# A decoder layer on one core: turning the normalized tokens of self attention through memory and VectorE blocks instead of TensorE turns

## The chip, the cores and the metric

The kernel runs on one core of a Trainium2 chip. The metric is the device time of one execution in microseconds (us). Three runs of the kernel before gave 3795.77, 3797.29 and 3797.58 us, so the median is 3797.29 us. The core's engines are named as in the profile: PE is TensorE (matmuls; PEld are its weight loads), DVE is VectorE, ACT is ScalarE, POOL is GpSimd and SP is SyncE, which issues most DMAs. A name with a q behind it (SPq) is the engine's instruction queue.

## What is computed

One decoder layer on 32 batches of 128 tokens with 512 columns, all in float32: self attention, cross attention and a mixture of experts, each on a layer-normalized input and each added to its input. The change touches the input of self attention alone:

```python
def _layernorm(x, axis=-1, eps=1e-05):
    m = jnp.mean(x, axis=axis, keepdims=True)
    v = jnp.var(x, axis=axis, keepdims=True)
    return (x - m) / jnp.sqrt(v + eps)
...
q = (x @ Wq).reshape(b, t, 2 * H, HD).transpose(0, 2, 1, 3) * scaling
k = (x @ Wk).reshape(b, t, 2 * H, HD).transpose(0, 2, 1, 3)
v = (x @ Wv).reshape(b, t, H, 2 * HD).transpose(0, 2, 1, 3)
scores = jnp.einsum('bhqd,bhkd->bhqk', q, k)
...
x = x + _L0_attn_ref(_layernorm(x, axis=-1), ...)
```

The three products with Wq, Wk and Wv sum over the 512 columns of x. TensorE sums over partitions, so the normalized tokens, which are made with a token on each partition, must be turned until the columns lie on the partitions.

## The kernel before

Self attention is the first of the kernel's stages. It goes over the 32 batches in 64 steps, two for each batch. A step n belongs to the batch and head half steps[n] (at most n // 2 and n % 2) and does, in the order of the program text: the turned maxima and half of the sums of the step before (`turn_maxima`, `sums`), the scores of this step and their row maxima (`maxima`), one quarter of the query and key projections of the next pair of batches (`queries_and_keys(g + 1, k)`, with g, k = divmod(n, 4)), the exponentials of the step before, the weighted values of two steps before, and then in odd steps the value projection of one later batch (`values`) and in even steps the output projection of an earlier one (`leave`).

The input is prepared further ahead. For batch b = 2(g + 2) + k // 2, an even step measures mean and variance (`measure`, L56 to L60 on DVE, L62 and L66 on POOL). The following odd step normalizes it (`normalize`, one ACT instruction, L87), turns it (`turn_in`) and loads the x of batch b + 2 (`load`, L151). So the batches 4 to 31 are turned in the 28 odd steps 1, 3, up to 55. Batches 0 to 3 are turned before the steps begin, in a section whose order is written out by hand. `turn_in` makes four TensorE transposes of 128x128 into a PSUM tile (`turn4`, L95) and copies the result to `hT` on ACT (L207). The tiles `xin`, `h` and `hT` have two buffers each.

PSUM is handed out by `banks`, four tiles in rotation (`psum`, bufs=4). Each request takes the tile that was requested four before, and so waits until that one has been read. An odd step requests, in this order: the turned maxima (L291), two for the scores (L251), one for the projections (L220), two for the exponentials (L308), one for the weighted values (L333), one for the value projection (L238) and one for the turn (L95). An even step has the output projection (L405) in place of the last two.

Behind the hand-written section the order on each engine is made by the tile framework's scheduler from its own estimates, not by the program text alone. The changed program is built by the same scheduler. An engine takes its instructions strictly in that order, and so does the queue of SP, on which an issue that waits holds back all the issues behind it.

The changed parts and their lines are: `turn4` (L89 to L96, shared with cross attention), the weight loads (L168 to L180), `normalize` and `turn_in` (L193 to L207), and the calls of `measure`, `normalize`, `turn_in` and `load` in the hand-written section (L471 to L476) and in the loop over the steps (L507 to L518).

Of the kernel before, what the change touches and what calls it, by code (L numbers as in the profile page):

```python
# [10 lines left out]
F32 = mybir.dt.float32  # L11
# [7 lines left out]
P = 128  # L19
E = 512  # L20
EC = E // P
# [14 lines left out]
class Common:  # L36
# [49 lines left out]

        self.nc.scalar.activation(out, src, AF.Identity, bias=down, scale=rstd)  # L87

    def turn4(self, src, order=range(EC)):  # L89


        tr = self.banks()[:, 0, :].rearrange("p (c x) -> p c x", c=EC)
        cols = src.rearrange("p (c x) -> p c x", c=EC)
        for c, n in enumerate(order):
            self.nc.tensor.transpose(tr[:, c, :], cols[:, n, :], self.ident)  # L95
        return tr  # L96
# [15 lines left out]
            call(*args)  # L112


def self_attention(cm, x, x1_d, Wq, Wk, Wv, Wo, lq1, lk1, lq2, lk2, heads, heads_in, beside):

# [11 lines left out]
    nc, tc, bank = cm.nc, cm.tc, cm.banks  # L130
    B = x.shape[0]
    H, D, G = 16, 32, 2
    CP = 2
    ROW = (16, 0)
    with ExitStack() as ctx:
# [7 lines left out]
        pj2 = early.enter_context(tc.tile_pool(name="a_pj2", bufs=2))  # L143

        xin, xres = {}, {}

        def load(b, queue=nc.sync):

            if b < B:
                xin[b] = pj2.tile([P, E], F32, name="xin")  # L150
                queue.dma_start(out=xin[b], in_=x[b])  # L151
# [10 lines left out]
        for b in range(G):  # L162
            load(b, both[b % 2])
        w = {
            name: (wp if name == "wo" else pj).tile([P, EC, E], F32, name=name)
            for name in ("wk", "wq", "wv", "wo")
        }
        for oc in range(EC):  # L168
            for name, src, queue in (("wk", Wk, nc.sync), ("wq", Wq, both[oc < 2])):
                queue.dma_start(  # L170
                    out=w[name][:, :, ts(oc, P)],
                    in_=src[:, ts(oc, P)].rearrange("(c p) m -> p c m", p=P),
                )
            if oc == 0:
                nc.sync.dma_start(out=heads, in_=heads_in)
        vecs = wp.tile([P, 4, 16], F32, name="lam_vecs")
        for i, src in enumerate((lq1, lq2, lk1, lk2)):
            nc.sync.dma_start(out=vecs[:, i, :], in_=src.partition_broadcast(P))
        for name, src in (("wv", Wv), ("wo", Wo)):
            nc.sync.dma_start(out=w[name], in_=src.rearrange("(c p) m -> p c m", p=P))  # L180

        begun = wp.tile([P, 1], F32, name="a_begun")
        nc.scalar.activation(begun, cm.mhalf[:, 0:1], AF.Exp)
# [1 line left out]
        hT, qT, kz, k1, vs = {}, {}, {}, {}, {}  # L185
        last, last_v = {}, [None]
        h, sc_of, qm, expd, u, o, an = {}, {}, {}, {}, {}, {}, {}

        def measure(b):
            if b < B:  # L190
                h[b] = cm.moments(pj2, xin[b], "a_")

        def normalize(b):  # L193
            if b < B:
                rstd, down = h[b]
                h[b] = pj2.tile([P, E], F32, name="h")
                cm.shifted(h[b], xin.pop(b), rstd, down)

        def turn_in(b):

            if b >= B:
                return
            g, i = divmod(b, G)
            if i == 0:
                hT[g] = pj2.tile([P, EC, G * P], F32, name="hT")
            tr = cm.turn4(h.pop(b))
            nc.scalar.copy(hT[g][:, :, ts(i, P)], tr)  # L207

        def queries_and_keys(g, oc):

# [220 lines left out]
        for b in range(G):  # L431
# [8 lines left out]
            out=causal, in_=causal, compare_op=ALU.is_ge, fill=NEG, base=0,  # L440
# [32 lines left out]
        for b in range(G):  # L473
            turn_in(G + b)
            load(2 * G + b)
        first.close()  # L476
        steps = [(b, cp) for b in range(B) for cp in range(EC // CP)]
        for n in range(len(steps) + 5):
            g, k = divmod(n, 2 * G)
            if n == len(steps) - 2 * G:  # L480
                early.close()
            at = {ago: steps[n - ago] for ago in range(6) if 0 <= n - ago < len(steps)}
            if 1 in at:
                turn_maxima(*at[1])
                sums(*at[1], 0)
            if 0 in at:
                maxima(*at[0])
            queries_and_keys(g + 1, k)
            if 1 in at:
                exponentials(*at[1])  # L490
                sums(*at[1], 1)
            if 2 in at:
                weigh(*at[2])
            if k % 2:
                values(g + 1, k // 2)
            elif 5 in at:
                leave(at[5][0])
            if 2 in at:
                divide(*at[2])
                if at[2][1]:  # L500
                    finish(at[2][0])

            def behind():

                return tc.issue_after(last[at[0]].ins) if 0 in at else nullcontext()

            b = (g + 2) * G + k // 2  # L507
            if k % 2 == 0:
                if 3 in at:
                    with behind():  # L510
                        norms(at[3][0])
                measure(b)
                if 4 in at:
                    load_again(at[4][0])
            else:
                normalize(b)
                turn_in(b)
                load(b + G)  # L518
                if 4 in at:
                    with behind():  # L520
                        scale_out(at[4][0])
                    turn_out(at[4][0])
            if n in beside:
                beside[n]()


class CrossAttention:
# [108 lines left out]
    def measure(self, b):  # L636
        q = self.sided[b, "q", 0] = self.pi.tile([P, E], F32, name="xq0", bufs=2)
        self.scale[b] = self.cm.moments_by_sums(self.pi, self.src[b, "q"], q, "x_")
# [575 lines left out]
class Shared:  # L1214
# [4 lines left out]
    G = 4  # L1219
# [482 lines left out]
def decoder_kernel(  # L1702
# [5 lines left out]
    nc = tc.nc  # L1708
    B = x.shape[0]
# [5 lines left out]
    dram = ctx.enter_context(tc.tile_pool(name="dram", bufs=1, space=DRAM))  # L1715
    psum = ctx.enter_context(tc.tile_pool(name="psum", bufs=4, space=PSUM))
    cm = Common(tc, const, psum)
    heads = const.tile([P, 8], F32, name="heads")
# [5 lines left out]
    half_eid = const.tile([P, 2], I32, name="half_eid")  # L1724

    x1_d = dram.tile([B, P, E], F32, name="x1_d")
    h3_d = dram.tile([T, E], F32, name="h3_d")
    h3T_d = dram.tile([B, P, EC, P], F32, name="h3T_d")
    table_ds = [dram.tile([(NX * B + 2) * P, 2], F32, name=f"table_d{i}") for i in range(2)]
# [6 lines left out]
    with tc.tile_pool(name="x_w", bufs=1, side="right") as x_w:  # L1736
        rest = x_w.tile([P, E], F32, name="rest")
        nc.gpsimd.memset(rest, 0.0)
        routing = Routing(cm, x_w, table_ds, B)
        cross = CrossAttention(cm, x_w, x1_d, x2_d, h3_d, h3T_d, ctx_in, routing)  # L1740
        cross.plan(lambda: s_w.load(), lambda: shared.load(0))
        x_ctx = ExitStack()

        def begin():
            cross.begin(
                x_ctx.enter_context(
                    tc.tile_pool(name="x_in", bufs=2, side="right", reuse_waits="tile")
                )
            )
            cross.advance(7)  # L1750

        n = 2 * B
        beside = {
            12: lambda: cross.load_weights(
                xWq, xbq, xWk, xbk, xWv, xbv, xWo, xbo, cos, sin, rotT, gate_w
            ),
            20: lambda: cross.prepare(heads),
            28: routing.prepare,
            n - 4: begin,
        }  # L1760

        for i, count in enumerate((4, 4, 5, 2, 2, 2, 2)):
            beside[n - 3 + i] = lambda count=count: cross.advance(count)
        self_attention(cm, x, x1_d, aWq, aWk, aWv, aWo, lq1, lk1, lq2, lk2, heads, heads_in, beside)
        s_w_pool = ctx.enter_context(tc.tile_pool(name="s_w", bufs=1, reuse_waits="tile"))
        s_w = SharedWeights(cm, s_w_pool, sw_gate, sw_up, sw_down)
        s_h_pool = ctx.enter_context(tc.tile_pool(name="s_h", bufs=2, reuse_waits="tile"))
        shared = Shared(cm, s_h_pool, h3T_d, sum_d, out)
        x_out = ExitStack()
        p2 = x_out.enter_context(tc.tile_pool(name="x_p2", bufs=2, reuse_waits="tile"))  # L1770
        cross.run(p2)
        x_ctx.close()
        s_pool = x_out.enter_context(tc.tile_pool(name="s_p", bufs=1, reuse_waits="tile"))
        shared.use(s_pool, s_w)
        en = mybir.EngineType
        in_order = {en.PE, en.DVE, en.Activation, en.Pool}
        todo = [lambda: cross.rest(2)] * 34 + [
            lambda: routing.tiles(eid, fresh, rows, used, usual, mixed),
            lambda: routing.halves(half, half_eid),
            lambda: nc.sync.dma_start(out=sum_d[T : T + P, :], in_=rest),  # L1780
        ]

        def between():
            if todo:
                todo.pop(0)()

        EARLY = 3  # L1790
        with tc.manual_schedule(engines=in_order):
            for g in range(EARLY - 1):
                shared.group(g, False, between)
            while todo:
                between()
# [42 lines left out]
    for i in range(2):  # L1838
        b = done // 2
        nc.sync.dma_start(  # L1840
            out=out[ts(i, b)].rearrange("b (p r) e -> (b p) (r e)", r=4),
# [57 lines left out]
```

## Time and profile before

| what | value |
|---|---|
| median of three runs | 3797.29 us |
| the profiled execution | 3800.08 us |
| its span, first to last instruction | 3798.3 us |
| mean granted TensorE clock in it | 0.992 |
| first L257 of step 0 / of step 11 | 40.8 us / 163.3 us |
| last turn (L95) of self attention | about 672 us |
| L95 MATMUL on h in self attention, 128 of them | 273 ns each (median) |
| L207 ACT copy to hT, 32 of them | 574 ns each |
| L87 ACT normalization of xin, 32 of them | 816 ns each |
| L56, L58, L60 DVE moments | 694, 181 and 153 ns each |

The span is the time between the first and the last instruction of one execution; the profiled execution took 1.8 us more than its span and 2.8 us more than the median. Self attention takes about the first 720 us of it. In the views below, a time is the start in us from the beginning of the span, followed by the duration in us; merged rows stand for several instructions (x8), and the bracket at the end gives the idle time before the row on its engine and the instruction that ended it. A float32 matmul of the program appears as two MATMUL rows.

### The profile page before, as it was taken

The numbers are of one execution on the slowest core, as the hardware profiler recorded it, in microseconds if no ns is written. First come the engines' busy times: TensorE is split into PE (matmuls) and PEld (weight loads), VectorE is DVE, ScalarE is ACT, GpSimd is POOL, SyncE is SP. The second block draws the span as 40 slices with busy tenths as digits, with TensorE's granted clock in tenths as the row PEclk, the third lists the DMA queues.
The fourth block names the chain that finished last, engine by engine and source line by source line (L and its number), as shares of the span: only waits on it lengthen the run. The fifth ranks groups of instructions, "written<-read, shape, count | busy, mean of one in ns | idle before, by whom it ended". The sixth has DMA issues, their size and how long they took to land. (4 is left out here: it accounts for less than half of the span.)

```text
span 3798.3 us, 59896 instructions
## 1 busy us (share of the span) xinstructions
PE 3717.0 (98%) x19060; PEld 1967.8 (52%) x19060; DVE 2677.8 (70%) x5402; ACT 2076.4 (55%) x5616; POOL 1917.2 (50%) x2154
## 2 busy tenths in 40 slices
PE   8999999899999999999999999999999999999999
PEld 5666666534444444444445555555555555555444
DVE  4888888877777778787326777777777777776111
ACT  6989998847677676776402444444444444443000
POOL 3555455545777777777424554555555555553000
PEclk9999999999999999999999999999999999999999
DMA  3111110121221111111135565656566665564210
GB/s 113 34 35 35 35 37 30 39 83 49 62 60 42 51 51 51 48 49 40 56 110 169 128 164 134 166 121 164 122 156 142 150 150 141 135 172 81 89 56 33
DMA packets 146548, 340.25 MB, mean 90 GB/s; under 512 B 28976, under 2 KB 33776, under 8 KB 146160
## 3 DMA queue, kind: packets, MB, share of 16 engines
q1 hardware_dynamic: 89408, 227.75, 18.8%
q0 software_dynamic: 55616, 107.79, 15.4%
q8 instruction: 154, 2.52, 0.3%
q14 instruction: 170, 1.39, 0.1%
q10 hardware_dynamic: 1200, 0.79, 0.1%
HBM read 574.59 MB, written 102.17 MB: 178 GB/s over the span
## 5 line engine op out<-in xcount | busy, mean ns | idle before, releaser
L694 DVE TENSOR_REDUCE nm<-ps 128x2 f32<-128x1024 f32 x512 | 610.6, 1214 | 113.2 <-PE ps L690 106.8
L717 ACT ACTIVATE xp<-ps 128x1024 f32<-128x1024 f32 x512 | 505.8, 1021 | 264.5 <-PE ps L690 202.7
L1644 POOL DMA_INDIRECT sum_d<-e_out,e_into x192 | 309.9, 1614 | 562.6 <-ACT e_out L1641 438.4
L713 PE MATMUL ps<-xqn,xk 32*128 32x512 f32 x2048 | 528.9, 621 | 20.7 <-ACT xp L717 19.1
L1637 PE MATMUL ps<-wd,e_guT 128*128 128x512 f32 (+1 forms) x1152 | 526.9, 593 | 0.3 <-ACT e_guT L1627 0.3
L690 PE MATMUL ps<-xk,xq 32*128 32x512 f32 x2048 | 526.9, 631 | 0.1
L1584 DVE STREAM_TRANSPOSE e_xT<-e_xr 64x256 f32<-64x256 f32 x800 | 499.5, 624 | 18.9 <-DMA e_xr<-h_d,e_run_of 10.7
L1609 DVE STREAM_TRANSPOSE e_guT<-e_gu 32x96 f32<-32x96 f32 x1600 | 477.7, 299 | 25.2
L1569 POOL DMA_INDIRECT e_xr<-h_d,e_run_of x400 | 413.8, 1035 | 159.7 <-issue 150.0
L1598 PE MATMUL ps<-wg,e_xT 128*128 128x352 f32 x1536 | 486.7, 459 | 0.0
L1598 PE MATMUL ps<-wu,e_xT 128*128 128x352 f32 x1536 | 485.7, 459 | 0.0
L1627 ACT COPY e_guT<-e_turned 32x96 f32<-32x96 f32 (+1 forms) x1600 | 407.1, 254 | 25.1 <-DVE e_turned L1620 3.9
L1598 PEld LDWEIGHTS ps<-wg,e_xT 128*128 128x128 f32 x1536 | 289.7, 189 | 217.8 <-issue 94.5
L278 ACT ACTIVATE s<-s,a_nm 128x128 f32<-128x128 f32 x1024 | 395.7, 396 | 5.2 <-DVE a_nm L264 5.2
L1598 PEld LDWEIGHTS ps<-wu,e_xT 128*128 128x128 f32 x1536 | 291.8, 190 | 162.6
L1641 ACT ACTIVATE e_out<-ps,e_weight 128x512 f32<-128x512 f32 x200 | 137.4, 687 | 411.8 <-PE ps L1637 409.5
L1637 PEld LDWEIGHTS ps<-wd,e_guT 128*128 128x128 f32 (+1 forms) x1152 | 218.5, 190 | 228.2 <-issue 188.5
L1602 ACT ACTIVATE e_act<-ps 128x352 f32<-128x352 f32 x200 | 92.6, 463 | 412.7 <-PE ps L1598 412.7
L713 PEld LDWEIGHTS ps<-xqn,xk 32*128 32x128 f32 x2048 | 169.0, 184 | 285.5 <-ACT xp L717 124.5
L1603 DVE TENSOR_TENSOR e_gu<-e_act,ps 128x352 f32<-128x352 f32 x200 | 104.1, 521 | 274.6 <-ACT e_act L1602 274.1
L728 PE MATMUL ps<-xp,v 128*32 128x512 f32 x2048 | 233.0, 595 | 7.9 <-ACT xp L717 7.9
L1031 POOL DMA_INDIRECT table_d<-entry,at x192 | 202.4, 1054 | 64.0 <-issue 52.9
(310 smaller groups left out, 5575.4 us busy)
## 6 DMA issues: line engine op xcount, KB each, us to landing
wg<-in_L_ffn_w_gate_dram SPq DMA_DIRECT2D x192, 704.0 KB
wu<-in_L_ffn_w_up_dram SPq DMA_DIRECT2D x192, 704.0 KB
wd<-in_L_ffn_w_down_dram SPq DMA_DIRECT2D x192, 576.0 KB
wd<-in_L_ffn_w_down_dram SPq DMA_DIRECT2D x192, 128.0 KB
xg<-in_L_ffn_w_gate_dram SPq DMA_DIRECT2D x16, 704.0 KB
xu<-in_L_ffn_w_up_dram SPq DMA_DIRECT2D x16, 704.0 KB
xd<-in_L_ffn_w_down_dram SPq DMA_DIRECT2D x16, 576.0 KB
xres<-in_x_dram SPq DMA_DIRECT2D x32, 256.0 KB
```

What stands on the lines that cost most here:

```text
L278: nc.scalar.activation(s[:, j, c, side, :], s[:, j, c, side, :], AF.Exp, bias=nm[n][:, side, at : at + 1], accum_out=sm[n][:, to : to + 1],)
L690: self.nc.tensor.matmul(sc[:, i, :], q[rows, ts(c, P)], k[rows, :], start=True, stop=True)
L694: self.nc.vector.tensor_reduce(at[:, self.ROW[side], 2 * pair : 2 * pair + 2], sc, AX.X, ALU.max, negate=True)
L713: self.nc.tensor.matmul(sc[:, i, :], k[rows, ts(c, P)], q[rows, :], start=True, stop=True)
L717: self.nc.scalar.activation(e, sc, AF.Exp)
L1569: self.cm.nc.gpsimd.indirect_dma_start(out=xr[:, t, :], out_offset=None, in_=self.h3_d.rearrange("t (h f) -> (t h) f", h=self.R), in_offse ...
L1584: self.cm.nc.vector.transpose(to[ts(w, half), :, v], xr[ts(v, half), w])
L1598: nc.tensor.matmul(pgu[lanes, half, 0:M], t[:, c, lanes], w[:, c, :], start=c == 0, stop=c == EC - 1,)
L1609: self.cm.nc.vector.transpose(t[ts(q, 32), :, ts(s, 32)], self.part(q, 3)[ts(s, 32)])
L1627: self.cm.nc.scalar.copy(t[ts(q, 32), 0:n, ts(s, 32)], z[ts(s, 32), q - half, 0:n])
L1637: nc.tensor.matmul(py[lanes], t[:n, c, lanes], wd[:n, c, :], start=c == 0, stop=c == last)
L1644: nc.gpsimd.indirect_dma_start(out=self.sum_d[:, :], out_offset=bass.IndirectOffsetOnAxis(ap=into, axis=0), in_=y[:, :], in_offset=None, b ...
```

## The change

The normalized tokens of batches 4 to 31 no longer go to TensorE to be turned. ACT writes them with the columns in another order: column q*128 + 4f + c goes to place q*128 + 32c + f. That row is stored in a new array in memory, `h_d` (one DMA for each batch, 256 KB), and read back with four DMAs of 64 KB, one for each q, in runs of 128 elements (512 bytes): partition 32q + i of the tile `h_runs` receives the runs of the tokens i, 32 + i, 64 + i and 96 + i. One DVE transpose of 32x32 blocks then gives `hT`, in which partition p holds the columns 4p to 4p + 3 instead of p, 128 + p, 256 + p and 384 + p. The rows of Wk, Wq and Wv are loaded in the same order, and batches 0 to 3, which are still turned on TensorE, read every fourth column. In the loop, the even step now normalizes and sends, and the odd step receives and measures the next batch.

```diff
-    def turn4(self, src, order=range(EC)):
+    def turn4(self, src, order=range(EC), strided=False):
         tr = self.banks()[:, 0, :].rearrange("p (c x) -> p c x", c=EC)
-        cols = src.rearrange("p (c x) -> p c x", c=EC)
+        cols = src.rearrange("p (x c) -> p c x" if strided else "p (c x) -> p c x", c=EC)
...
-                    in_=src[:, ts(oc, P)].rearrange("(c p) m -> p c m", p=P),
+                    in_=src[:, ts(oc, P)].rearrange("(p c) m -> p c m", p=P),
...
-        for name, src in (("wv", Wv), ("wo", Wo)):
-            nc.sync.dma_start(out=w[name], in_=src.rearrange("(c p) m -> p c m", p=P))
+        nc.sync.dma_start(out=w["wv"], in_=Wv.rearrange("(p c) m -> p c m", p=P))
+        nc.sync.dma_start(out=w["wo"], in_=Wo.rearrange("(c p) m -> p c m", p=P))
...
-        def turn_in(b):
-            if b >= B:
-                return
+        def turned(b):
             g, i = divmod(b, G)
             if i == 0:
                 hT[g] = pj2.tile([P, EC, G * P], F32, name="hT")
-            tr = cm.turn4(h.pop(b))
-            nc.scalar.copy(hT[g][:, :, ts(i, P)], tr)
+            return hT[g][:, :, ts(i, P)]
+
+        def turn_in(b):
+            nc.scalar.copy(turned(b), cm.turn4(h.pop(b), strided=True))
+
+        def send(b):
+            if b >= B:
+                return
+            rstd, down = h[b]
+            t = pj2.tile([P, E], F32, name="h")
+            cm.shifted(
+                t.rearrange("p (q c f) -> p q f c", q=4, c=EC),
+                xin.pop(b).rearrange("p (q f c) -> p q f c", q=4, c=EC), rstd, down,
+            )
+            nc.sync.dma_start(out=h_d[b], in_=t)
+            h[b] = pj2.tile([P, 4, P], F32, name="h_runs")
+            for q in range(4):
+                nc.sync.dma_start(
+                    out=h[b][ts(q, 32)],
+                    in_=h_d[b][:, ts(q, P)].rearrange("(t i) r -> i t r", i=32),
+                )
+
+        def receive(b):
+            if b < B:
+                nc.vector.transpose(
+                    turned(b).rearrange("p c (t i) -> p c t i", i=32),
+                    h.pop(b).rearrange("p t (c f) -> p c t f", c=EC),
+                )
...
         for b in range(G):
             turn_in(G + b)
             load(2 * G + b)
+        measure(2 * G)
         first.close()
...
-                measure(b)
+                send(b)
                 if 4 in at:
                     load_again(at[4][0])
             else:
-                normalize(b)
-                turn_in(b)
+                receive(b)
+                measure(b + 1)
                 load(b + G)
...
+    h_d = dram.tile([B, P, E], F32, name="h_d")
```

More of the change, by code (lines that the diff above doesn't have):

```diff
@@ L112, in run, with self_attention @@
             call(*args)
-def self_attention(cm, x, x1_d, Wq, Wk, Wv, Wo, lq1, lk1, lq2, lk2, heads, heads_in, beside):
+def self_attention(cm, x, x1_d, h_d, Wq, Wk, Wv, Wo, lq1, lk1, lq2, lk2, heads, heads_in, beside):
     nc, tc, bank = cm.nc, cm.tc, cm.banks
@@ L1763, in decoder_kernel @@
             beside[n - 3 + i] = lambda count=count: cross.advance(count)
-        self_attention(cm, x, x1_d, aWq, aWk, aWv, aWo, lq1, lk1, lq2, lk2, heads, heads_in, beside)
+        self_attention(cm, x, x1_d, h_d, aWq, aWk, aWv, aWo, lq1, lk1, lq2, lk2, heads, heads_in, beside)
         s_w_pool = ctx.enter_context(tc.tile_pool(name="s_w", bufs=1, reuse_waits="tile"))
```

## The prediction

> **What bounds the kernel now.** I read the page first, for the busiest engine:
>
> ```profile
> PE 3717.0 (98%) x19060; PEld 1967.8 (52%) x19060; DVE 2677.8 (70%) x5402; ACT 2076.4 (55%) x5616; POOL 1917.2 (50%) x2154
> ```
>
> PE is busy 98% of the span, and the chain of waits that ended last is PE work too, but a modelled busy time doesn't say what a step costs. So I read the busy time by stretches of self attention next (start and end, length, then busy us and instructions of PE, PEld, DVE, ACT, POOL, then granted clock, DMA share, GB/s). The first stretch holds steps 0 to 10, the second steps 11 to 54.
>
> ```profile
> 40.00:163.00 123.00, 118.38 (x947) 77.52 (x939) 94.90 (x140) 108.50 (x416) 54.85 (x63) 0.96 0.08 25
> 163.00:661.00 498.00, 497.34 (x4092) 318.15 (x4092) 415.71 (x614) 450.73 (x1712) 258.79 (x260) 1.00 0.11 35
> ```
>
> In the second, PE never pauses, ACT is busy 91% and DVE 83%. The timeline of PE over two steps shows where the time goes, even step first, odd step second:
>
> ```profile
> 406.37 1.17 PE L308 MATMUL ps<-qm,k 32*128 32x128 f32 x32
> ...
> 412.08 0.38 PE L291 MATMUL ps<-ident,a_nm 128*128 128x128 f32 x2
> 412.39 1.15 PE L251 MATMUL ps<-kz,qT 32*128 32x256 f32 x16
> 413.46 1.99 PE L220 MATMUL ps<-hT,wk 128*128 128x256 f32 x8
> ...
> 417.11 1.17 PE L308 MATMUL ps<-qm,k 32*128 32x128 f32 x32
> ...
> 422.82 0.60 PE L95 MATMUL ps<-ident,h 128*128 128x128 f32 x4
> 423.26 0.38 PE L291 MATMUL ps<-ident,a_nm 128*128 128x128 f32 x2
> 423.57 1.79 PE L251 MATMUL ps<-kz,qT 32*128 32x256 f32 x16
> 425.30 1.99 PE L220 MATMUL ps<-hT,wk 128*128 128x256 f32 x8
> ...
> 428.95 1.17 PE L308 MATMUL ps<-qm,k 32*128 32x128 f32 x32
> ```
>
> From L308 to L308 the even step takes 10.74 us and the odd one 11.84. The difference of 1.10 has two parts: the turns move L291 back by 423.26 - 422.82 = 0.44, and from L251 to L220 the odd step takes 1.73 where the even one takes 1.07, so 0.66 of waiting inside work that counts as busy. The ACT timeline says for what:
>
> ```profile
> 423.61 0.57 ACT L242 COPY v<-ps 128x512 f32<-128x512 f32 x1
> 424.07 0.64 ACT L368 ACTIVATE sq<-at 128x512 f32<-128x512 f32 x1
> 424.61 0.57 ACT L207 COPY hT<-ps 128x512 f32<-128x512 f32 x1
> ```
>
> With the turn among the PSUM requests, the second score tile of L251 is the one that the value copy (L242) empties at 424.18, and the tile of L220 is the one that the hT copy (L207) empties at 425.18; L220 starts 0.12 later.
>
> **What a step without the turn costs is in the trace.** The last turn is in step 55. Row maxima (L264) of steps 55 to 59:
>
> ```profile
> 664.38 2.35 DVE L264 TENSOR_REDUCE a_nm<-s 128x8 f32<-128x1024 f32 x2
> 675.81 2.35 DVE L264 TENSOR_REDUCE a_nm<-s 128x8 f32<-128x1024 f32 x2
> 686.96 2.35 DVE L264 TENSOR_REDUCE a_nm<-s 128x8 f32<-128x1024 f32 x2
> 697.68 2.35 DVE L264 TENSOR_REDUCE a_nm<-s 128x8 f32<-128x1024 f32 x2
> 708.47 2.34 DVE L264 TENSOR_REDUCE a_nm<-s 128x8 f32<-128x1024 f32 x2
> ```
>
> Steps 55 and 56 together take 22.58 us, steps 57 and 58, with the same projections but no turn, 21.51. So a turn costs **1.07 us** with its waits, which agrees with the 1.10 above.
>
> **The change part by part.**
>
> *Removed turns, steps 11 to 55.* 23 odd steps at 1.07 are **-24.6 us**. The next tile in line is then that of L220 behind the value copy. Without 0.44 and 0.66, L220 would start at 424.20, and the copy ends at 424.18, driven by the exponentials of the same step: a tie, so the wait is gone to within 0.1. Bounds: 0.44 a step (-10.1) if the bank wait stays, 1.10 (-25.3).
>
> *Steps 0 to 10.* Here the built order of the changed program matters, and the diff alone doesn't show it. Nothing holds the front end back any more except `xin`, since `h` leaves for memory. The scheduler places all moments up to batch 31 ahead of the scores of step 11: 26 instead of the 7 that the trace counts in this stretch. It places 28 normalizations there instead of 7, and the first six receives. DVE gains 19 x (0.694 + 0.181 + 0.153) = 19.5 and 6 transposes of 0.711 (the row L392, same shape, same block transpose) = 4.3, so 94.9 + 23.8 = 118.7 of 123. ACT gains 21 x 0.816 = 17.1 less 6 hT copies of 0.574 = 3.4, so 108.5 + 13.7 = 122.2 of 123. PE, which would save 5 x 1.07 = 5.4 here, isn't the bound of this stretch any more; ACT is. At full ACT use it takes 122.2 (-0.8), at the 90.5% of the second stretch 135.0 (+12). I take the middle, **+6**. Bounds: -5.4 if both engines' work hides, and the slow rival below.
>
> *The normalization itself* keeps 512 elements, but writes neighbours 128 bytes apart. No ACT row does that. Nearest: DVE's reciprocal at L745 reads 128x32 at such a step in 343 ns, and L955 the same count side by side in 353. So I take 0.816, with 1.63 (double) as the upper bound: 28 x 0.816 = +22.8, all inside the full ACT stretch. On this the Trainium skill speaks against the change: "SBUF — State Buffer", section "Door 1: The DMA port swizzle", says that each access crossing to a new 16-byte line pays a penalty, and every write here does. It gives ScalarE no figure; no ACT row here shows it. By the rule the sum would lie toward the upper bound, by the reciprocal rows at zero.
>
> *The DMAs.* Each batch adds a store and four reads to SP's queue, all at 0.33 us an issue (the row of xin): 1.65 a batch against 22.58 in which SP now issues three. A load is read 2.57 us after its issue (406.04 issue of xin, 408.61 its L56), so a batch is back about 2.57 + 4 x 0.33 + 2.57 = 6.5 us after ACT, ahead of its receive in the built order. In the later steps the reads are issued one pair of batches early, some 45 us ahead, so a DVE wait on them costs nothing. Behind a waiting read on SP stand the store of x1 and loads of xin and xres; xres is needed about four steps later, xin is the slow rival's subject. Traffic: 28 x 0.5 MB over some 680 us is 21 GB/s more in a stage that moves 35. Cost 0; if the cover goes, the slow rival.
>
> *The receives in the later steps* (22 x 0.711 = 15.6) replace 19 moments (19.5) on DVE, which was idle 17% anyway. They come in twos right before L293, whose result PE needs 3.6 us after L291; two transposes take 1.4. Cost 0, at worst 11 x 1.4 = +15.6.
>
> *Start.* 16 weight loads on PE now read every fourth column: 141 ns each before, at most doubled +2.3, at least 0; I take **+1**. The value weights come in longer rows: 0.
>
> Sum: -24.6 + 6 + 1 = -17.6, so the profiled 3800.1 would become 3782.5; the median of the runs lies 2.8 below the profiled execution, which gives **3780**.
>
> **Rivals.**
> *The bank wait stays.* If ACT reaches the value copy later than PE reaches L220, only 0.44 a step is saved: -10.1 + 6 + 1 = -3, 3794. For: the tie of 0.02 us. Against: steps 57 and 58. A doubled normalization ends in the same place: 122.2 + 22.8 = 145 against 123 is +22, less 24.6, about 3796. Together 0.20.
> *The run ahead is free.* 28 x 1.07 = -30 from all steps: 3767. For: DVE waits 7.4 us on L291 in step 1. Against: ACT's sum. 0.08.
> *Slower: DVE stands before x that hasn't come.* 26 moments now go through a two-buffer loop of load, moments, POOL, ACT and load, and their loads stand on SP behind stores that wait for ACT.
>
> ```profile
> DVE a_ln_stats L56 <- DMA xin<-in_x_dram: 16.4, 19, 1.1
> ```
>
> In the second stretch each moment already waits 0.86 us (16.4 / 19), harmless at 83% DVE. In the first stretch DVE would have 4.3 to spare. The whole becomes a loss when a moment waits more than (24.6 - 1 + 4.3) / 26 = 1.07 us. At a full load time of 2.57 it is 118.7 + 66.8 - 123 - 23.6 = +39; halfway, 1.8 us each, +19: **3816**. For: the load time is 2.5 times the break-even. Against: with DVE late, loads have landed. 0.15.
> *That it doesn't do what it says:* the built PE order is the old one less 28 groups of four turns, so this is out.
>
> **How the numbers follow.** Forecast 0.57, with its own range 3768 to 3791; rivals 0.20, 0.08 and 0.15 as above. A difference of 0.2% is 7.6 us, which is what I take as the limit of telling: faster means below 3789.7, slower above 3804.9. Faster: 0.55 + 0.08 + 0.02 = 0.65; same 0.20; slower 0.15. For 8 in 10 the range goes from 3767 to 3806: it takes in the free run-ahead and the unchanged cases and leaves out most of the slow one.
>
> **What would show it.** L264 to L264 over two steps at 21.5 us in steps 12 to 54; L251 to L220 at 1.07 in both; no L95 between 60 and 672 us; step 11's scores at 163 + 6 us; the new L87 form at 0.82 us; L56 waits on xin under 1 us each in the first stretch. A row of L87 above 1.2 us, a first stretch over 145 us or any L220 waiting for v would prove me wrong.

## The result, and the profile after

Six runs of the changed kernel gave 3819.77 to 3825.24 us, median 3821.89; six runs of the kernel before beside them gave 3795.77 to 3797.58, median 3796.75. The ratio is 1.0068, with a 95% interval of 1.0055 to 1.0081. So the change made the kernel slower by 0.7%, where the forecast was 3780 and a gain. The profiled execution of after has a span of 3819.8 us, 21.5 more than before. (The medians are 25.1 apart; the profiled execution of before was itself 3.3 us above its median.)

Lines 208 and later of the program have moved. The scores on DVE are now L283 (before L257), the row maxima L290 (L264), the projections L246 (L220), the score matmuls L277 (L251), the exponentials L341 (L315), the value copy L268 (L242). New are the store L219, the reads L222 and the block transpose L230.

From the page of after, its busy times, and from its 40 slices the granted clock:

```profile
PE 3708.7 (97%) x18948; PEld 1960.0 (51%) x18948; DVE 2688.4 (70%) x5430; ACT 2074.8 (54%) x5588; POOL 1918.2 (50%) x2154
PEclk8899999989999999999999999999999999999999
```

PE has 112 matmuls fewer, as the change says (28 batches, four turns each), and is busy 8 us less, yet the span is longer. The sum of the busy times doesn't hold the answer. The busy times by stretches of after do (columns as in the prediction: start and end, length, busy us and instructions of PE, PEld, DVE, ACT and POOL, granted clock, DMA share, GB/s):

```profile
40.00:163.00 123.00, 97.10 (x720) 64.03 (x719) 84.02 (x147) 98.24 (x326) 48.35 (x72) 0.83 0.32 101
222.00:661.00 439.00, 438.33 (x3710) 280.38 (x3708) 376.70 (x530) 391.47 (x1536) 222.36 (x202) 1.00 0.12 36
```

In the first stretch every engine did less than before: PE 97.1 us against 118.4, DVE 84.0 against 94.9, ACT 98.2 against 108.5, and the clock fell from 0.96 to 0.83. Nobody was full; all waited for each other. From 222 us on PE has no pause and the clock is 1.00. The DVE timeline of after dates the steps: L283 marks the scores of steps 0, 3, 6, 7, 10 and 11 here, L290 the row maxima of steps 15 and 54 to 57.

```profile
41.22 2.36 DVE L283 TENSOR_TENSOR s<-ps,causal 128x1024 f32<-128x1024 f32 x2 [5.36 <-PE ps L277]
...
80.28 2.36 DVE L283 TENSOR_TENSOR s<-ps,causal 128x1024 f32<-128x1024 f32 x2 [2.06 <-PE ps L277]
...
121.69 2.35 DVE L283 TENSOR_TENSOR s<-ps,causal 128x1024 f32<-128x1024 f32 x2
142.21 2.35 DVE L283 TENSOR_TENSOR s<-ps,causal 128x1024 f32<-128x1024 f32 x2
...
182.08 2.35 DVE L283 TENSOR_TENSOR s<-ps,causal 128x1024 f32<-128x1024 f32 x2
204.32 2.35 DVE L283 TENSOR_TENSOR s<-ps,causal 128x1024 f32<-128x1024 f32 x2
...
257.87 2.35 DVE L290 TENSOR_REDUCE a_nm<-s 128x8 f32<-128x1024 f32 x2
...
679.37 2.34 DVE L290 TENSOR_REDUCE a_nm<-s 128x8 f32<-128x1024 f32 x2
690.16 2.35 DVE L290 TENSOR_REDUCE a_nm<-s 128x8 f32<-128x1024 f32 x2
700.88 2.35 DVE L290 TENSOR_REDUCE a_nm<-s 128x8 f32<-128x1024 f32 x2
711.67 2.35 DVE L290 TENSOR_REDUCE a_nm<-s 128x8 f32<-128x1024 f32 x2
```

Against the same instructions of before, whose times stand in brackets:

- Step 0 starts 0.4 us later (41.22; 40.83).
- Step 11 starts 41.0 later (204.32; 163.31). So steps 0 to 10 cost 40.6 us more.
- Step 15 has its row maxima 47.0 later (257.87; 210.84): 6.0 more.
- Step 55 has them 25.8 later (690.16; 664.38): steps 15 to 54 gained 21.2, which is **1.06 us for each of the 20 turns** that are gone there.

So the late steps do what was predicted, and steps 0 to 14 lose more than twice as much (46.6). In the late steps the PE timeline of after now shows both kinds of step alike, even step first, odd step second:

```profile
406.82 1.15 PE L277 MATMUL ps<-kz,qT 32*128 32x256 f32 x16
407.90 1.99 PE L246 MATMUL ps<-hT,wk 128*128 128x256 f32 x8
...
411.55 1.17 PE L334 MATMUL ps<-qm,k 32*128 32x128 f32 x32
...
417.57 1.15 PE L277 MATMUL ps<-kz,qT 32*128 32x256 f32 x16
418.67 1.99 PE L246 MATMUL ps<-hT,wk 128*128 128x256 f32 x8
...
422.32 1.17 PE L334 MATMUL ps<-qm,k 32*128 32x128 f32 x32
```

From L277 to L246 it is 1.08 and 1.10 us, and L334 to L334 takes 10.77: the wait for the value copy is gone with the turn.

What the first steps wait for stands in the waits of after from 40 to 222 us (us in total, times, longest):

```profile
DVE a_ln_stats L56 <- DMA xin<-in_x_dram: 43.4, 21, 5.2
...
ACT h L87 <- POOL a_ln_down L66: 23.1, 6, 6.5
```

And one turn of the loop behind these waits, in the timeline of step 2 of after, the engines together:

```profile
65.96 2.35 ACT L87 ACTIVATE h<-xin,a_ln_down,a_ln_rstd 128x512 f32<-128x512 f32 x2
...
67.69 0.42 SPq L151 DMA_DIRECT2D xin<-in_x_dram  x1
...
70.68 0.69 DVE L56 BATCH_NORM_STATS2 a_ln_stats<-xin 128x6 f32<-128x512 f32 x1 [3.32 <-DMA xin<-in_x_dram]
...
72.58 0.26 POOL L66 TENSOR_SCALAR a_ln_down<-a_ln_mv,a_ln_rstd 128x1 f32<-128x1 f32 x1
72.88 1.27 ACT L87 ACTIVATE h<-xin,a_ln_down,a_ln_rstd 128x512 f32<-128x512 f32 x1 [3.71 <-POOL a_ln_down L66]
...
75.82 1.28 ACT L87 ACTIVATE h<-xin,a_ln_down,a_ln_rstd 128x512 f32<-128x512 f32 x1 [1.67 <-POOL a_ln_down L66]
76.90 1.95 ACT L341 ACTIVATE e<-ps 128x1024 f32<-128x1024 f32 x2
...
78.00 2.98 PE L277 MATMUL ps<-kz,qT 32*128 32x256 f32 x16 [7.89 <-ACT e L341]
```

Read it as a circle. ACT normalizes and thereby frees an `xin` buffer; SP loads the next x into it (67.69); DVE stands idle for 3.32 us until it has come (70.68, 3.0 after the issue); POOL finishes the moments (72.84); ACT, which has stood idle for 3.71, normalizes (72.88). Then the same again for the other buffer. The exponentials of the step (L341 at 76.90) stand behind these normalizations in ACT's queue and PE waits 7.89 us for them (78.00), though nothing about them needs the later batches. Three of the four longest steps are those with the longest waits of ACT: 17.7 us from step 2 to 3 (5.4 of them ACT's waits above), 20.5 from 6 to 7, 22.2 from 10 to 11.

### The profile page after: what moved, and what is told of

The parts are those of the page before. It is cut to its first block, busy times and chain, and to the rows that moved or that the text cites. A ratio compares the mean times of both kernels' runs of the same rounds, so it can differ in the third digit from the quotient of the medians.

```text
span 3819.8 us, 60075 instructions
## 1 busy us (share of the span) xinstructions
PE 3708.7 (97%) x18948; PEld 1960.0 (51%) x18948; DVE 2688.4 (70%) x5430; ACT 2074.8 (54%) x5588; POOL 1918.2 (50%) x2154
## 5 line engine op out<-in xcount | busy, mean ns | idle before, releaser
L1611 DVE STREAM_TRANSPOSE e_xT<-e_xr 64x256 f32<-64x256 f32 x800 | 498.6, 623 | 17.7 <-DMA e_xr<-h_d,e_run_of 9.5
L1654 ACT COPY e_guT<-e_turned 32x96 f32<-32x96 f32 (+1 forms) x1600 | 407.1, 254 | 25.1 <-DVE e_turned L1647 3.9
```

Source lines behind the costliest of these rows:

```text
L1611: self.cm.nc.vector.transpose(to[ts(w, half), :, v], xr[ts(v, half), w])
L1654: self.cm.nc.scalar.copy(t[ts(q, 32), 0:n, ts(s, 32)], z[ts(s, 32), q - half, 0:n])
```

## The experiments

The theory after this reading: the loss is the **run-ahead**. The scheduler, freed from the `h` buffers, sets the normalizations of 21 further batches, and their moments, among the first twelve steps, and in-order queues make the steps wait for the two-buffer loop. (That they stand there is in the trace; that it was the `h` buffers which had kept them back is read from the program, and no run tries it.) Rivals: the strided ACT write (a longer L87), the DMA traffic itself, the receives on DVE, or the turn through memory being dear in any order.

### e1_held: the measurement held back

```diff
             else:
                 receive(b)
-                measure(b + 1)
+                with behind():
+                    measure(b + 1)
                 load(b + G)
```

> The changed kernel with one edit: in each odd step the moments of the next batch are queued behind that step's row maxima on DVE, so they can't run ahead of the steps; the store, the four reads, the block transposes and the strided normalization stay. Theory (the run-ahead in steps 0 to 14 loses about 47 us and the 28 removed turns are worth 1.07 us each): 3797 - 30 + 1 = 3768, between 3762 and 3777, with steps 0 to 10 back at about 120 us and every pair of later steps at 21.5. Rival A (the strided normalization, 1.27 us instead of 0.82, is what costs): it is still there 28 times, so over 3800. Rival B (the way through memory, with SP's queue full of it, is what costs): over 3810.

Measured: 3912.65 us, ratio 1.0301 [1.0284, 1.0318]. The run-ahead is gone, but two steps now take 27.1 us (row maxima at 400.50 and 427.59) instead of 21.5. Waits of e1_held between 163 and 661 us, and then its timeline of one odd step:

```profile
DVE hT L230 <- DMA h_runs<-h_d: 66.6, 19, 4.9
```

```profile
407.25 0.32 SPq L219 DMA_DIRECT2D h_d<-h  x1
...
409.26 1.74 SPq L222 DMA_DIRECT2D h_runs<-h_d  x4
...
412.74 0.71 DVE L230 STREAM_TRANSPOSE hT<-h_runs 128x512 f32<-128x512 f32 x1 [3.26 <-DMA h_runs<-h_d]
413.37 2.31 DVE L283 TENSOR_TENSOR s<-ps,causal 128x1024 f32<-128x1024 f32 x2
```

From the store's issue to the transpose it is 5.5 us, and the scheduler set the transpose ahead of the scores L283, so DVE stands idle for 3.3 us with the whole step behind it. The trip through memory was free in after under the cover of the run-ahead; here nothing covers it. The rest of the 5.6 us that a pair loses wasn't separated: PE waits in other places too, and the granted clock of this stretch is 0.93. The experiment exchanged one wait for another and so did not price the run-ahead; e6_receive_held takes this wait away.

### e2_plain_write: ACT writes side by side

```diff
             cm.shifted(
-                t.rearrange("p (q c f) -> p q f c", q=4, c=EC),
-                xin.pop(b).rearrange("p (q f c) -> p q f c", q=4, c=EC), rstd, down,
+                t, xin.pop(b), rstd, down,
             )
```

> The changed kernel with the normalization writing its columns in their old order, side by side; everything behind it is unchanged, so the columns reach the projections in a wrong order and the output is not the reference's. The run-ahead stays. Theory (run-ahead): L87 back to 0.82 us takes at most 28 x 0.45 = 12.6 off, so 3809 to 3822. Rival A (strided writes are the cost): below 3797. Rival B: no difference from the changed kernel, 3820.

Measured: 3815.36, ratio 1.0046 [1.0029, 1.0063]. L87 falls from 1270 to 809 ns, and the waits of L56 on x stay (37.3 us in 19 between 40 and 222 us, where after has 43.4 in 21). The strided write is worth 3821.9 - 3815.4 = 6.5 us, a quarter of the loss: real, and not the main cause.

### e3_deep_xin: five buffers for x

```diff
-                xin[b] = pj2.tile([P, E], F32, name="xin")
+                xin[b] = pj2.tile([P, E], F32, name="xin", bufs=5)
```

> The changed kernel with five buffers of xin instead of two; the run-ahead stays possible and may go further. Theory in its narrow form (what costs is DVE standing before an x that its two-buffer loop has not loaded yet, 43 us of L56 waits): these waits fall below 15 us in all and the time to 3775 to 3800. If instead the sheer extra work in the first steps is too much for DVE and ACT, whatever the buffers: 3812 to 3830.

Measured: 3794.53, ratio 0.9991 [0.9982, 1.0001], so 27 us faster than after and not told apart from before. The waits of L56 on x fall to 9.3 us in 7 between 40 and 222 us. The first stretch of e3_deep_xin:

```profile
40.00:163.00 123.00, 102.97 (x744) 66.91 (x737) 92.86 (x172) 112.80 (x360) 60.53 (x92) 0.88 0.43 137
```

ACT does 112.8 us instead of 98.2, but PE only 103.0 against 118.4 in before: more normalizations fit in, the steps still come late. Step 11 starts at 184.04, 20 earlier than in after and still 20.7 later than in before. What waits now is POOL's L62 on ACT's L87 (32.8 us in 10, between 40 and 222 us) and DVE's L58 on POOL's L66 (14.7 in 10): behind the `xin` buffers the loop meets the next ones, those of the moments. How these 20.7 us divide between such waits and PE's lower clock (0.88) wasn't tried separately.

### e4_back_to_pe: the run-ahead with the turns kept

```diff
-                t.rearrange("p (q c f) -> p q f c", q=4, c=EC),
-                xin.pop(b).rearrange("p (q f c) -> p q f c", q=4, c=EC), rstd, down,
+                t, xin.pop(b), rstd, down,
...
-            h[b] = pj2.tile([P, 4, P], F32, name="h_runs")
-            for q in range(4):
-                nc.sync.dma_start(...)
+            h[b] = pj2.tile([P, E], F32, name="h_back")
+            nc.sync.dma_start(out=h[b], in_=h_d[b])
...
-                nc.vector.transpose(...)
+                turn_in(b)
```

> The run-ahead and the store to memory kept, but the row is written in the old order, read back in one plain DMA and turned by four TensorE transposes as before the change (they read every fourth column); no block transpose on DVE, no strided write. Theory: the loss of the run-ahead without the gain of the removed turns, so 3797 + 40, between 3825 and 3855. If the block transposes on DVE, the four strided reads or the strided write are what costs, the time is 3797 to 3808.

Measured: 3847.85, ratio 1.0133 [1.0116, 1.0150]. Here neither the strided write nor the block transpose exists, the four turns are back on TensorE (reading every fourth column), and of the change only the way through memory with its run-ahead is left. It costs 3847.9 - 3798.5 = 49 us by itself; L56 waits on x 42.2 us in 21 between 40 and 222 us. All of it is lost early: step 15 has its row maxima 48.8 later than before (259.68; 210.84), and so has step 55 (713.19; 664.38). The difference between this kernel and after, 26 us, is what taking the turns off TensorE gives, net of the longer ACT write and the transposes on DVE. So the change's loss is measured by itself and its gain as a difference; whether the loss is the run-ahead or the way through memory is left to e9_send_held and e12_only_send_held.

### e6_receive_held: the receive held too

```diff
-                receive(b)
-                measure(b + 1)
+                with behind():
+                    receive(b)
+                    measure(b + 1)
```

> The held kernel with the block transpose (L230) queued behind the row maxima of its odd step as well, so that DVE meets it about 5 us later than the reads need. Theory now (the run-ahead loses time in the first steps; in the held kernel the way through memory lost it instead, because DVE stood 3.3 us before the read row in front of the scores in each odd step): the waits of L230 on h_runs disappear, pairs of steps take 21.5 to 22 us, 3766 to 3785. Rival A (the strided normalization on ACT is what keeps the held kernel long): it stands at the end of an ACT-heavy odd step as before, so pairs stay at 22.5 or more and the time over 3800. Rival B (the way through memory costs by itself, wherever the transpose stands): over 3850.

Measured: 3800.12, ratio 1.0005 [0.9995, 1.0014]. No wait of L230 on its reads is left, and the run-ahead is gone, but two late steps take 22.78 us (row maxima at 398.37 and 421.15), as many as before the change. The wait that now ends last, from the waits of e6_receive_held between 163 and 661 us, and its timeline:

```profile
PE ps L431 <- ACT qT L257: 20.9, 21, 1.0
```

```profile
411.44 1.29 ACT L87 ACTIVATE h<-xin,a_ln_down,a_ln_rstd 128x512 f32<-128x512 f32 x1
...
412.53 0.79 ACT L252 ACTIVATE kz<-ps,a_keep 128x256 f32<-128x256 f32 x2
413.21 0.38 ACT L257 ACTIVATE qT<-ps 128x256 f32<-128x256 f32 x1
...
413.64 3.70 PE L431 MATMUL ps<-wo,anT 128*128 128x512 f32 x8 [1.00 <-ACT qT L257]
```

The normalization (1.29 us) now runs ahead of the copies of the projections (L252, L257), and PE, which needs the tile that L257 empties, waits 1.0 us in each pair of steps: as much as a turn. The gain is eaten on ACT. The numbers are those that the expectation gave to its rival A (pairs of 22.5 or more, over 3800); whether it is the length of the strided write or its place, e8_one_ahead_dve and e9_send_held tell.

### e7_one_ahead: the trip to memory two steps earlier

```diff
-                send(b)
+                send(b + 1)
...
-                receive(b)
-                measure(b + 1)
-                load(b + G)
+                with behind():
+                    receive(b)
+                    measure(b + 2)
+                load(b + 1 + G)
```

Before the loop, `send(2 * G)`, `load(3 * G)` and `measure(2 * G + 1)` are added.

> As the run before, and moments, normalization, store and reads one batch earlier, so the read row has more than 20 us. Theory: no L230 wait at all, the same 3766 to 3785 as with the transpose held alone; if it is more than 5 us faster than that run, the distance was still too short there. Rival A: as there, over 3800.

Measured: 3801.20, ratio 1.0009 [0.9999, 1.0018], the same as e6_receive_held, with the same wait of L431 on L257 (20.9 us in 21). The distance between store and transpose is not what holds it.

### e8_one_ahead_dve: the strided access moved from ACT to DVE

As e7_one_ahead, with the write and the transpose changed:

```diff
-                t.rearrange("p (q c f) -> p q f c", q=4, c=EC),
-                xin.pop(b).rearrange("p (q f c) -> p q f c", q=4, c=EC), rstd, down,
+                t, xin.pop(b), rstd, down,
...
-                    h.pop(b).rearrange("p t (c f) -> p c t f", c=EC),
+                    h.pop(b).rearrange("p t (f c) -> p c t f", c=EC),
```

> As the run before, but the normalization writes its columns side by side and the block transpose reads every fourth column instead; the output is the same. Prices: L87 falls from 1.27 to 0.82 us, L230 rises from 0.71 to 0.9 to 1.4. Theory: PE is the bound and ACT has about 1 us to spare in two steps, so this is worth 0 to 8 us against the run before. Rival A (ACT's strided writes are a main cost): 12 us or more faster than the run before.

Measured: 3803.93, ratio 1.0015 [1.0006, 1.0025]. ACT's L87 takes 0.80 us and DVE's transpose, which now reads every fourth element, 1.18 instead of 0.70. The time doesn't fall, and PE's wait for L257, which is L256 here, stays (23.7 us in 21), so it isn't the length of the ACT write that makes it. What ACT gains DVE seems to pay. ACT's squares wait for the sum that POOL makes from DVE's results, in e7_one_ahead and then in e8_one_ahead_dve between 163 and 661 us:

```profile
ACT sq L394 <- POOL at L389: 35.8, 21, 1.7
```

```profile
ACT sq L393 <- POOL at L388: 46.1, 21, 2.2
```

That is 0.49 us more in each pair of steps, as much as the transpose grew by.

### e9_send_held: the normalization behind the exponentials

As e6_receive_held, and in the even step the send is held behind the second exponential, which the loop keeps in `last_e`:

```diff
-                nc.scalar.activation(
+                last_e[0] = nc.scalar.activation(
...
-                send(b)
+                with tc.issue_after(last_e[0].ins) if last_e[0] else nullcontext():
+                    send(b)
```

> As the first run of these four (moments and transpose held), and the normalization queued on ACT behind the exponentials of the even step, where ACT waits 1.57 us for PE, instead of the odd step, where the value copy and the squares already stand. Theory: all 28 turns are saved at 1.07 us and nothing is given back, 3797 - 30 + 1 = 3768, between 3764 and 3774, the fastest of the four. If only 0.44 a turn can be saved: 3785 to 3792.

Measured: 3774.43, ratio 0.9938 [0.9922, 0.9955]: **faster than both kernels**, by 23 us than before and by 47 than after. Its two stretches:

```profile
40.00:163.00 123.00, 116.55 (x996) 76.36 (x996) 103.75 (x147) 112.41 (x427) 55.85 (x62) 1.00 0.18 53
163.00:661.00 498.00, 495.50 (x4134) 315.14 (x4133) 458.99 (x668) 457.36 (x1763) 263.63 (x272) 1.00 0.20 59
```

In the first stretch the clock is 1.00 and PE does 996 matmuls, against 720 in after and 947 in before. The same work as in after is spread over the steps. Its timeline at one step:

```profile
414.53 1.92 ACT L341 ACTIVATE e<-ps 128x1024 f32<-128x1024 f32 x2
...
416.33 1.30 ACT L87 ACTIVATE h<-xin,a_ln_down,a_ln_rstd 128x512 f32<-128x512 f32 x1
```

L87 is as long as in after, but stands where PE needs nothing from ACT at once: it follows the exponentials instead of preceding the copies. Two late steps take 21.7 us (row maxima at 400.48 and 422.20), and step 11 starts at 156.50, 6.8 ahead of before. The way through memory with all its traffic, the strided write and the receives on DVE are all still here, so none of these rivals makes after slow by itself. From e6_receive_held, which has the same instructions, it differs by the hold alone: the place of the normalization is worth 26 us.

### e10_deep_plain: five buffers and the plain write

The edits of e2_plain_write and e3_deep_xin together.

> Five buffers of xin and the side-by-side normalization together, run-ahead kept; the columns come in a wrong order, so the output is not the reference's. What is left of the loss in the first twelve steps with five buffers (step 11 at 184 us instead of 163) is either ACT's work (28 normalizations of 1.27 us there) or the run-ahead's order itself. If ACT's work: 28 x 0.45 = 12.6 off, 3780 to 3785, step 11 at about 171 us. If the order: 3790 to 3795, step 11 still past 180 us.

Measured: 3789.83, ratio 0.9979 [0.9970, 0.9989]. Step 11 starts at 180.58, 3.5 earlier than with five buffers alone, and still 17 later than in before. Relieving ACT of its longer write doesn't remove the rest of the loss. What is left is the run-ahead, but not its order alone: between 40 and 222 us POOL's L62 still waits for ACT's L87 (28.5 us in 7), L56 for x (8.2 in 4), and the first stretch has a clock of 0.90. These parts weren't separated.

### e11_send_held_dve: e9_send_held with the access moved to DVE

The edits of e9_send_held and the two of e8_one_ahead_dve.

> The fastest version (moments, transposes and normalizations held) with side-by-side writes on ACT (0.81 us instead of 1.29) and block transposes that read every fourth column on DVE (1.18 us instead of 0.70); the output is the same. If ACT is what keeps its pairs of steps at 21.7 instead of 21.5: 3768 to 3773. If DVE, which is 92% busy there, is nearer the bound: 3775 to 3795.

Measured: 3784.18, ratio 0.9964 [0.9950, 0.9978], 10 us slower than e9_send_held. DVE is busy 462.8 of 498 us in the late stretch, ACT 446.0. As in e8_one_ahead_dve, ACT's wait for POOL's sum grows, from 38.3 us in 22 to 48.7 in 22, which is about the 10 us that are lost.

### e12_only_send_held: the one edge alone

After, with the hold on `send` of e9_send_held and nothing else: receive and measure run free.

> The changed kernel with the normalization alone queued behind the exponentials of the even step; moments and transposes are left to the scheduler. If the run-ahead goes through the two buffers of xin, this one edit must stop all of it, since a buffer comes free only every second step: step 11 before 160 us and 3768 to 3780. If the moments or the transposes needed their own hold, DVE waits on xin or h_runs come back: over 3785.

Measured: 3779.59, ratio 0.9949 [0.9933, 0.9966], 42 us faster than after. Step 11 starts at 164.47 instead of 204.32, 4 later than the expectation's limit of 160, and each L56 that waits for x waits 0.8 us (20.5 us in 25 between 40 and 720 us) instead of 2. Of everything that was changed against after, this edge on a single instruction per pair of steps brings 42 of the 47 us.

## Why the prediction was wrong

**The step that failed is "Steps 0 to 10 ... I take the middle, +6".** It measured +40.6. The prediction had seen in the built order that the normalizations and moments move into this stretch, and it had named the two-buffer loop as its slow rival. But it priced the step by filling engines: DVE 118.7 of 123 and ACT 122.2 of 123, hence a stretch a little longer at worst. The work came out near this sum; the filling did not. From the scores of step 0 to those of step 11, after has

```profile
41.22:204.32 163.10, 127.59 (x913) 81.36 (x914) 110.84 (x201) 127.68 (x428) 71.61 (x100) 0.85 0.32 101
```

DVE did 110.8 us and ACT 127.7, but in 163.1: they were 68% and 78% full, where ACT had been taken at 90.5% to 100%. The waits of the loop make the difference: an issue of x at 67.69 and the next one into the same buffer at 74.61, 6.9 us a turn at this place, with DVE and ACT each standing in it and the steps' own work behind them. e4_back_to_pe shows the run-ahead without the gain at +49, e3_deep_xin that more `xin` buffers take 27 back, and e12_only_send_held that one order edge takes 42 back.

**The term of steps 11 to 55, -24.6, came out at -16.3**: step 11 starts 41.0 later than before and step 57 has its row maxima 24.7 later (711.67; 686.96). Steps 11 to 14 lost 6.0 where the sum had a gain of 2.1; the last normalization of the run-ahead stands in step 11 (213.97).

**The slow rival** (3816, a chance of 0.15) was the right mechanism with too small a chance. Its break-even was 1.07 us of waiting per moment, its own guess 1.8; measured were 43.4 / 28 = 1.55. Its stretch, 118.7 + 26 x 1.8 = 165.5, lies close to the 163.1 measured, in part by luck, since it counted DVE's waits only. ACT's waits on POOL in the same circle, 23.1 us, and the fallen clock were not in it. The argument against it, "with DVE late, loads have landed", was wrong because the load is not issued until ACT has normalized: a late DVE makes the load late too.

**The turn at 1.07 us, removed in steps 15 to 54: right**, 1.06 measured. L277 to L246 at 1.08 and 1.10 was foreseen as 1.07, and the rival that the bank wait stays is out.

**The normalization at 0.816 us: mis-sized**, 1.27 measured, within the bounds of 0.816 and 1.63. The groups of after, from 30 to 720 us (us in total, mean ns of one, idle before and what ended it):

```profile
L87 ACT ACTIVATE h<-xin,a_ln_down,a_ln_rstd 128x512 f32<-128x512 f32 x28 | 33.5, 1270 | 23.1 <-POOL a_ln_down L66 23.1
L230 DVE STREAM_TRANSPOSE hT<-h_runs 128x512 f32<-128x512 f32 x28 | 19.8, 707 | 7.7 <-PE ps L264 7.7
```

DVE's reciprocal rows, by which I chose, said nothing about an ACT write. On this point the Trainium skill ("SBUF — State Buffer", "Door 1: The DMA port swizzle", a penalty for every access that crosses to a new 16-byte line) pointed the right way, and the row puts the size at 0.46 us an instruction. By e2_plain_write the write is worth 6.5 us. "All inside the full ACT stretch" was wrong along with the stretch.

**The block transpose at 0.711: right**, 707 ns. **Receives at 0 in the later steps**: right in after, where they come long before they are needed; a receive set ahead of the scores cost 3.3 us each in e1_held.

**The DMAs at 0: right for after, under its cover.** The estimated round trip of 6.5 us was 5.5 in e1_held, and there, without the run-ahead, DVE waited for it in 19 of the odd steps between 163 and 661 us. In after the cover that made this term zero was the very run-ahead that made the other one dear. It takes no run-ahead, though: in e9_send_held, where the transpose stands later in its step, L230 waits 1.5 us in all between 163 and 661 us.

**The start, +1**: 0.4. The weight loads of the turns of batches 0 to 3 take 212 ns (median). The 141 ns of the prediction belong to the later batches; these same loads took 162 before, and their matmuls take 351 after 347. In e4_back_to_pe, where the later batches are turned with the same step of four, the load takes 198 ns instead of 141 and the matmul 283 instead of 273.

**The signs of being wrong that the prediction had set itself** all came: a row of L87 above 1.2 us (1.27), a first stretch over 145 us (163.1 from the scores of step 0 to those of step 11), and projections that wait for the value copy (PE's L246 on L268, 8.5 us in 4 between 40 and 222 us, none from there to 661).

## What to carry to other kernels

What limits how far a front end can run ahead is also part of the schedule: when a change removes such a limit, ask what the scheduler will now put in front of the urgent work, and price the stretch by the round trip of the loop that remains, not only by adding busy times to idle ones. Where the order turns out wrong, give the scheduler an edge (issue this after that) before giving it more buffers: five buffers brought 27 us here, one edge 42. And put new work on a nearly full engine right behind the instruction that others wait for, not before it: the same 1.3 us normalization cost PE 1.0 us a pair ahead of the copies and nothing that shows behind the exponentials.

## What the runs showed of the hardware

- An ACT instruction over 128x512 float32 that writes neighbours 128 bytes apart took 1.27 us, one that writes them side by side 0.81.
- A DVE block transpose of 128x512 float32 that reads every fourth element took 1.18 us, one that reads 32 neighbours in each run 0.70.
- The granted clock was lowest where PE stood idle most: 0.83 in the first stretch of after (PE idle 26 of 123 us), 0.88 with five buffers (20 of 123), and 0.93 in the late stretch of e1_held (67 of 498). There PE also computes more slowly (in after the L246 at 80.91 takes 3.78 us instead of 1.99), which a sum of durations from another stretch doesn't contain. But idle time alone doesn't settle the clock: it was 1.00 in the late stretch of e6_receive_held with 22 of 498 us idle, and in the first stretch 1.00 in e9_send_held with 6.5 us idle against 0.96 before with 4.6. What sets it wasn't tried. The late stretches of e1_held and e6_receive_held:

```profile
163.00:661.00 498.00, 431.36 (x3311) 272.76 (x3308) 344.37 (x535) 375.69 (x1419) 207.58 (x218) 0.93 0.16 50
```

```profile
163.00:661.00 498.00, 476.44 (x3968) 302.43 (x3970) 439.91 (x639) 441.71 (x1683) 250.93 (x262) 1.00 0.19 58
```

- Two DVE instructions (L378) took more than twice their time in some steps. The DVE and POOL timeline of e9_send_held, an odd and an even step:

```profile
406.33 2.32 POOL L344 TENSOR_SCALAR_AFFINE_SELECT e<-e 128x1024 f32<-128x1024 f32 x2
406.47 1.23 DVE L378 SCALAR_TENSOR_TENSOR o<-u,rs 128x256 f32<-128x256 f32 x1
407.62 1.30 DVE L378 SCALAR_TENSOR_TENSOR o<-u,nlam,rs 128x256 f32<-128x256 f32 x1
...
416.37 0.43 DVE L378 SCALAR_TENSOR_TENSOR o<-u,rs 128x256 f32<-128x256 f32 x1
416.71 0.48 DVE L378 SCALAR_TENSOR_TENSOR o<-u,nlam,rs 128x256 f32<-128x256 f32 x1
...
418.21 2.13 POOL L344 TENSOR_SCALAR_AFFINE_SELECT e<-e 128x1024 f32<-128x1024 f32 x2
```

Where they run beside POOL's select (L344) they take 1.23 and 1.30 us, where they run before it 0.43 and 0.48. That the select is the cause wasn't tried by itself.
